# One written order for the last unit of a quantized FFN layer, and a changed order in its first units

## The chip, the cores and the metric

The kernel runs on one core of a Trainium2 chip. The metric is the device time of one execution in microseconds (us); a lower time is better. Times of before are the median of 3 runs; a separate execution was profiled, and all rows below come from that one.

## The reference

Two layers of an adapted feed-forward network work on x, 8 batches of 128 tokens with 512 features. What matters here is the second half of the second layer: a gated feed-forward part whose weights are 4-bit integers with one scale for each output row and each group of 128 inputs.

```python
def dequant(q, s, g=G):                       # G = 128
    O, In = q.shape
    return (q.reshape(O, In // g, g).astype(s.dtype) * s[:, :, None]).reshape(O, In)
...
Wg, Wu, Wd = dequant(gate_q, gate_s), dequant(up_q, up_s), dequant(down_q, down_s)
gate_score = jax.nn.silu(jnp.einsum('bsh,ih->bsi', x, Wg))      # I = 1792, H = 512
intermediate = gate_score * jnp.einsum('bsh,ih->bsi', x, Wu)
return jnp.einsum('bsi,hi->bsh', intermediate, Wd)
...
x = x + _L1_ffn_ref(_L1_cond_ref(x, itok_B_0_23, ...), ...)
```

## The kernel before

Features lie on the 128 partitions and tokens along the free axis: a tile is 128 x 1024, and a half of it (512 tokens, called tb 0 or 1) fills one PSUM bank. The last layer starts from h, the output of the adapter in front of it. h is held as two parts, `hi` (ACT rounds it, L1237) and `lo` (DVE takes the rest, L1239), so that each product needs two matmuls. Its halves come in the order in which the adapter finishes them; the last is chunk 3 of the first 512 tokens.

The 1792 inner features are cut into 14 units f of 128 (`NF`). For each unit there are 4 gate groups (s = 0, k = 0 to 3), 4 up groups (s = 1) and 4 down groups (o = 0 to 3). As the scales belong to groups of 128 inputs, each group is a PSUM result of its own, scaled while it is read out:

- `gate_or_up` (L1320 on): a pair of banks (`pair`), two halves with `hi` and `lo`, so 4 matmuls (`summed`, L1301). The first of a sum is read out by ACT (`scaled`, L1307), the others by DVE, which adds to the sum (L1310). Gate groups 0 and 1 go into one sum, 2 and 3 into another, which POOL adds (`gate_added`).
- `silu` on ACT (L1368), the product with the up sum on POOL (`gated_q`), the rounded part `act_hi` on ACT (`first_bits`, L1377) and the rest `act_lo` on POOL (`rest`). Every POOL operation is recorded at the helper `added`, L1316.
- `down_group` (L1342 on): 4 matmuls of `act_hi` and `act_lo`; DVE adds the scaled result to x (L1310), or ACT writes it to y (L1307) and POOL adds y to x (`y_added`).

Down groups belong to the unit two back (`LAG` = 2). Everything is issued with `in_order`, so each engine's list is the order of the Python text; an engine waits at the head of its list. Four pairs of banks go round: a group's first matmul waits until the group four back has been read out.

Units 0 to 12 run whole (L1386 to L1415). Inside a unit: gate 0, silu of the unit before (only f = 1 and 2), gate 1 (in unit 0: gate 2), `gated_q` of the unit before, down 0, gate 2, then `first_bits` and `rest` of the unit before, gate 3, `gate_added`, down 1, up 0 to 2, down 3 (by ACT and POOL), silu, up 3, down 2. POOL also issues the loads of later weights (L1193, L1195) between its operations.

The last unit (f = 13, L1419 on) runs in halves, each group in one bank of a second pool of 8 (`single`): first all 8 groups of tb 0, with the down groups of unit 11 between them, then all 8 of tb 1, then the down groups of unit 12, then those of unit 13, first tb 0 and then tb 1. x[o] of each half is stored (L1488) after its down group of unit 13: five stores by SP and three by ACT.

Of the kernel before, what the change touches and what calls it, by code (L numbers as in the profile page):

```python
# [7 lines left out]
F32 = mybir.dt.float32  # L8
# [3 lines left out]
ALU = mybir.AluOpType  # L12

P = 128
NB = 8
T = 1024
TB = 512
NTB = T // TB
G = 32
# [3 lines left out]
KC = H // P  # L23
R = 16
# [4 lines left out]
NF = FF // P  # L29
# [5 lines left out]
WARM = 2  # L35
NS = H + NF * P
LAG = 2


@with_exitstack  # L40
def kernel(
# [25 lines left out]
    nc = tc.nc  # L67

    nc_mm = nc.tensor.matmul
    in_order = tc.keep_in_program_order  # L70
# [40 lines left out]
    x = [const.tile([P, T], F32, tag=f"x{k}", name=f"x{k}") for k in range(KC)]  # L111
# [228 lines left out]
    ready = {}  # L340
# [164 lines left out]
    acts = {}  # L505
# [359 lines left out]
    with ExitStack() as top:  # L865
# [233 lines left out]
        first, then, last = scaling(1)  # L1099
# [41 lines left out]
    for sign in (1, -1):  # L1141
        in_order(
            nc.gpsimd.affine_select(
                out=one, in_=one, pattern=[[-sign, P]], compare_op=ALU.is_ge,
# [7 lines left out]
    sg = early.tile([P, NF, 2, KC], F32, tag="sg", name="sg")  # L1152
    sd = early.tile([P, KC, NF], F32, tag="sd", name="sd")
# [15 lines left out]
    b1 = gather_b(early, "1", l_bm, b1_rows, H)  # L1169
# [31 lines left out]
    whole, halves = slice(0, T), [bass.ts(tb, TB) for tb in range(NTB)]  # L1201
# [61 lines left out]
    for m in two:  # L1263
# [4 lines left out]
            fresh={(1, 1)}, go_on={(0, 0)},  # L1268
# [23 lines left out]
    def pair(name: str):  # L1292
        return pairs.tile([P, NTB, TB], F32, tag="pair", name=name)


    sums = {}

    def summed(ps, w, src, at):
        for n, part in enumerate(src):
            in_order(  # L1300
                nc.tensor.matmul(ps, w, part[:, at], start=(n == 0), stop=(n == len(src) - 1))  # L1301
            )

    def scaled(to, ps, scale, plus=None):

        if plus is None:
            in_order(nc.scalar.activation(to, ps, AF.Identity, scale=scale))  # L1307
        else:
            in_order(
                nc.vector.scalar_tensor_tensor(  # L1310
                    to, ps, scale, plus, op0=ALU.mult, op1=ALU.add
                )
            )

    def added(to, a, b, op):
        in_order(nc.gpsimd.tensor_tensor(to, a, b, op))  # L1316

    def unit_tile(what: str, f: int, bufs: int, dtype=F32):
        return l1.tile([P, T], dtype, tag=what, name=f"{what}_{f}", bufs=bufs)

    def gate_or_up(f: int, s: int, k: int, at=whole, into=None):


        on_act = k == 0 or (s == 0 and k == 2)
        if on_act and (f, s, k) not in sums:
            sums[f, s, k] = unit_tile(f"sum{s}{k}", f, 2)
        to = sums[f, s, k - k % 2 if s == 0 else 0][:, at]
        w, src = ready["q", f][0][:, s, k, :], [part[k] for part in parts]
        if into is None:
            both = pair(f"gu{s}_q{f}_{k}")  # L1330
            for tb in range(NTB):
                summed(both[:, tb], w, src, halves[tb])
            ps = both.rearrange("p b s -> p (b s)")
        else:
            summed(into, w, src, at)
            ps = into
        scaled(to, ps, sg[:, f, s, k : k + 1], None if on_act else to)

    def gate_added(f: int, at=whole):
        added(sums[f, 0, 0][:, at], sums[f, 0, 0][:, at], sums[f, 0, 2][:, at], ALU.add)  # L1340

    def down_group(f: int, o: int, on_act=False, at=whole, into=None):  # L1342
        w, src, scale = ready["q", f][1][:, bass.ts(o, P)], acts["q", f], sd[:, o, f : f + 1]
        if into is None:
            both = pair(f"d_q{f}_{o}")
            for tb in range(NTB):
                summed(both[:, tb], w, src, halves[tb])
            ps = both.rearrange("p b s -> p (b s)")
        else:
            summed(into, w, src, at)  # L1350
            ps = into
        to = x[o][:, at]
        if on_act:
            if (f, o) not in ys:
                ys[f, o] = unit_tile("y", f"{f}_{o}", 2)
            scaled(ys[f, o][:, at], ps, scale)
        else:
            scaled(to, ps, scale, to)

    ys = {}  # L1360

    def y_added(f: int, o: int, at=whole):
        added(x[o][:, at], x[o][:, at], ys[f, o][:, at], ALU.add)

    def silu(f: int, at=whole):
        if ("sil", f) not in sums:
            sums["sil", f] = unit_tile("sil_q", f, 2)
        in_order(nc.scalar.activation(sums["sil", f][:, at], sums[f, 0, 0][:, at], AF.Silu))  # L1368

    def gated_q(f: int, at=whole):  # L1370
        if ("q", f) not in acts:
            acts["q", f] = [unit_tile(f"act_{w}", f, 3, F32R) for w in ("hi", "lo")]
        up = sums[f, 1, 0][:, at]
        added(up, up, sums["sil", f][:, at], ALU.mult)

    def first_bits(f: int, at=whole):
        in_order(nc.scalar.copy(acts["q", f][0][:, at], sums[f, 1, 0][:, at]))  # L1377

    def rest(f: int, at=whole):
        hi, lo = acts["q", f]  # L1380
        added(lo[:, at], sums[f, 1, 0][:, at], hi[:, at].bitcast(F32), ALU.subtract)
# [4 lines left out]
    for f in range(NF - 1):  # L1386
        d = f - LAG
        if d > 0 and d - 1 + QBUFS < NF:
            load_q(d - 1 + QBUFS)
        gate_or_up(f, 0, 0)  # L1390
        if 0 < f <= LAG:
            silu(f - 1)
        gate_or_up(f, 0, 1 if f else 2)
        if f:
            gated_q(f - 1)
        if d >= 0:
            down_group(d, 0)
        gate_or_up(f, 0, 2 if f else 1)
        if f:
            first_bits(f - 1)  # L1400
            rest(f - 1)
        gate_or_up(f, 0, 3)
        gate_added(f)
        if d >= 0:
            down_group(d, 1)
        for k in range(3):
            gate_or_up(f, 1, k)
        if d >= 0:
            down_group(d, 3, True)
            y_added(d, 3)  # L1410
        if f >= LAG:
            silu(f)
        gate_or_up(f, 1, 3)
        if d >= 0:
            down_group(d, 2)  # L1415
# [2 lines left out]

    in_pairs.close()  # L1419
    last = ctx.enter_context(  # L1420
        tc.tile_pool(name="last", bufs=8, space=bass.MemoryType.PSUM, reuse_waits="tile")
    )

    def single(name: str):
        return last.tile([P, TB], F32, tag="bank", name=name)

    def down_half(f: int, o: int, tb: int, on_act: bool):
        down_group(f, o, on_act, halves[tb], single(f"d_q{f}_{o}_{tb}"))

    def down_halves(f: int, o: int, on_act: bool):  # L1430
        for tb in range(NTB):
            down_half(f, o, tb, on_act)

    def y_halves_added(f: int, o: int):
        for at in halves:
            y_added(f, o, at)

    f = NF - 1

    def half_unit(s: int, k: int, tb: int):  # L1440
        gate_or_up(f, s, k, halves[tb], single(f"gu{s}_q{f}_{tb}_{k}"))

    at = halves[0]
    for s in range(2):
        for k in range(KC):
            half_unit(s, k, 0)
            if (s, k) == (0, 1):
                gated_q(f - 1)
            if (s, k) == (0, 2):
                first_bits(f - 1)  # L1450
                rest(f - 1)
            if (s, k) == (0, 3):
                gate_added(f, at)
            if k % 2 == 1:
                o = 2 * s + k // 2
                down_halves(f - LAG, o, o == 1)
                if o == 1:
                    y_halves_added(f - LAG, o)
            if (s, k) == (1, 0):
                silu(f, at)  # L1460
    gated_q(f, at)

    d, at = f - 1, halves[1]
    for k in range(KC):
        half_unit(0, k, 1)
    gate_added(f, at)
    half_unit(1, 0, 1)
    silu(f, at)  # L1470
    half_unit(1, 1, 1)
    first_bits(f, halves[0])
    rest(f, halves[0])
    half_unit(1, 2, 1)
    half_unit(1, 3, 1)
    gated_q(f, at)
    down_halves(d, 1, True)
    down_halves(d, 0, False)
    first_bits(f, at)
    rest(f, at)  # L1480
    y_halves_added(d, 1)
    down_half(d, 3, 0, True)
    y_added(d, 3, halves[0])
    down_half(d, 3, 1, False)
    down_halves(d, 2, False)

    def store(engine, o: int, tb: int):
        in_order(engine.dma_start(out=out[:, o, halves[tb]], in_=x[o][:, halves[tb]]))  # L1488

    for o in (1, 0, 2, 3):  # L1490
        down_half(f, o, 0, o == 1)
        if o == 1:
            y_added(f, o, halves[0])
        else:
            store(nc.sync, o, 0)
    for n, o in enumerate(range(KC)):
        down_half(f, o, 1, False)
        if n == 0:
            store(nc.scalar, 1, 0)
        store(nc.scalar if n % 2 else nc.sync, o, 1)  # L1500


# [94 lines left out]
```

## Time and profile before

| what | value |
|---|---|
| runs | 709.4, 709.48, 707.73 us (median 709.4) |
| profiled execution | 707.46 us |
| its span | 705.7 us, 6850 instructions |
| mean granted TensorE clock | 0.994 |
| last layer's first matmul to its last eviction | 532.31 to 701.68 us of the span |
| last store's data ends | about 704.05 us |

The span is what the trace covers; the profiled execution is 1.76 us longer. A row of the timeline gives start, duration, engine, line, operation, output <- inputs, count, and in brackets how long the engine was idle before it and what released it. PE is TensorE, PEld its weight loads, DVE VectorE, POOL GpSimd, ACT ScalarE, SP the engine that issues most DMAs. A row with x4 covers four operations: its duration runs from the first one's start to the last one's end. A matmul here takes 0.39 us, but the next one starts 0.2268 us after it, since they are pipelined. A few matmuls at the very end (behind 698.16) are missing from the trace.

### The profile page before, as it was taken

How to read it: one execution, taken by the hardware profiler on the slowest of the kernel's cores; microseconds unless marked ns; L12 is line 12 of the kernel's file. 1: busy time of each engine (PE TensorE's matmuls, PEld its weight loads, DVE VectorE, ACT ScalarE, POOL GpSimd, SP SyncE). 2: the span in 40 equal slices, each digit the busy share in tenths (PEclk: the TensorE clock that was granted, in tenths of full speed). 3: DMA queues.
4: the chain of work that ended last, by engine and by line, in shares of the span. 5: the costliest groups of instructions: out<-in, count | busy, mean ns of one | idle time of the engine just before them, and what ended most of it. 6: DMA issues, size and time to landing. Idle time of an engine off the chain costs nothing. (4 is left out here: it accounts for less than half of the span.)

```text
span 705.7 us, 6850 instructions
## 1 busy us (share of the span) xinstructions
PE 676.7 (96%) x2400; PEld 381.8 (54%) x2400; DVE 445.4 (63%) x636; ACT 185.3 (26%) x273; POOL 370.6 (53%) x324
## 2 busy tenths in 40 slices
PE   8999999999999899898899899999999999999993
PEld 3444444444444345565566564444436677788872
DVE  6545344346242678687696479452447788999985
ACT  1221121110100012322333320000024655565642
POOL 5357666140001072955865748025203889898885
PEclk9999999999999999999999999999999999999998
DMA  6501234030002010220200050004900120000003
GB/s 228 188 1 51 76 124 169 1 134 1 1 0 104 1 61 29 90 89 1 90 1 0 16 175 25 0 0 118 329 1 30 41 79 16 15 1 1 0 1 119
DMA packets 18333, 42.46 MB, mean 60 GB/s; under 512 B 3118, under 2 KB 4286, under 8 KB 18172
## 3 DMA queue, kind: packets, MB, share of 16 engines
q1 hardware_dynamic: 11628, 25.44, 10.2%
q0 software_dynamic: 5376, 14.49, 6.6%
q10 hardware_dynamic: 1296, 2.10, 0.8%
q8 instruction: 19, 0.31, 0.2%
q14 instruction: 14, 0.11, 0.1%
HBM read 39.93 MB, written 2.10 MB: 60 GB/s over the span
## 5 line engine op out<-in xcount | busy, mean ns | idle before, releaser
L1310 DVE SCALAR_TENSOR_TENSOR sum<-gu_q,sg,sum 128x1024 f32<-128x1024 f32 (+1 forms) x75 | 90.4, 1211 | 20.0 <-ACT sum L1307 15.3
L1301 PE MATMUL gu_q<-h_hi,wgu_q 128*128 128x512 f32 x224 | 88.8, 396 | 3.1 <-DVE x L1310 1.6
L1301 PE MATMUL gu_q<-h_lo,wgu_q 128*128 128x512 f32 x224 | 87.5, 390 | 0.3 <-DVE h_lo L1239 0.3
L1310 DVE SCALAR_TENSOR_TENSOR x<-d_q,sd,x 128x1024 f32<-128x1024 f32 (+1 forms) x51 | 54.3, 1086 | 4.0 <-POOL x L1316 4.0
L73 PE MATMUL p_f<-T_h,s_f 128*128 128x512 f32 x112 | 52.9, 603 | 2.2 <-DVE T_h L319 2.2
L1307 ACT ACTIVATE sum<-gu_q,sg 128x1024 f32<-128x1024 f32 (+1 forms) x45 | 47.3, 1056 | 23.3 <-PE gu_q L1301 23.2
L1316 POOL TENSOR_TENSOR sum<-sum,sum 128x1024 f32<-128x1024 f32 (+1 forms) x15 | 33.9, 2262 | 36.6 <-DVE sum L1310 36.0
L1301 PEld LDWEIGHTS gu_q<-h_hi,wgu_q 128*128 128x128 f32 x224 | 42.0, 188 | 17.4 <-DVE x L1310 4.6
L1301 PE MATMUL d_q<-act_hi,wd_q 128*128 128x512 f32 x112 | 44.7, 399 | 3.6 <-ACT y L1307 3.2
L1301 PEld LDWEIGHTS gu_q<-h_lo,wgu_q 128*128 128x128 f32 x224 | 42.1, 188 | 8.9 <-DVE h_lo L1239 0.6
L1301 PE MATMUL d_q<-act_lo,wd_q 128*128 128x512 f32 x112 | 44.0, 392 | 0.3 <-POOL act_lo L1316 0.3
L1316 POOL TENSOR_TENSOR act_lo<-sum,act_hi 128x1024 fp32r<-128x1024 f32 (+1 forms) x15 | 33.8, 2256 | 18.0 <-ACT act_hi L1377 16.7
L73 PE MATMUL p_c<-x,raw_c 128*128 128x512 f32 x88 | 42.7, 606 | 0.5 <-DMA x<-in_xT_dram 0.5
L73 PE MATMUL p_c<-T_x,raw_c 128*128 128x512 f32 x88 | 41.6, 594 | 0.2 <-DVE T_x L319 0.2
L73 PE MATMUL p_c<-T_x,s_c 128*128 128x512 f32 x88 | 41.2, 592 | 0.0
L570 DVE TENSOR_TENSOR act_c<-p_c,v_c 128x512 f32<-128x512 f32 x11 | 7.6, 691 | 52.3 <-PE p_c L73 52.3
L73 PE MATMUL p_f<-h,raw_f 128*128 128x512 f32 (+1 forms) x96 | 40.2, 541 | 0.1
L73 PE MATMUL d_f<-act_f,ds_f 128*128 128x512 f32 x84 | 36.6, 593 | 0.0
L73 PE MATMUL d_f<-act_f,wd_f 128*128 128x512 f32 x84 | 36.4, 592 | 0.0
L685 POOL TENSOR_TENSOR h<-h,dv_c 128x512 f32<-128x512 f32 x2 | 2.5, 1267 | 62.9 <-ACT dv_c L682 62.9
L1316 POOL TENSOR_TENSOR sum<-sum,sil_q 128x1024 f32<-128x1024 f32 (+1 forms) x15 | 33.9, 2261 | 2.7 <-ACT sil_q L1368 2.7
L1316 POOL TENSOR_TENSOR x<-x,y 128x1024 f32<-128x1024 f32 (+1 forms) x17 | 34.1, 2015 | 0.0
(276 smaller groups left out, 1265.3 us busy)
## 6 DMA issues: line engine op xcount, KB each, us to landing
raw_f<-in_f_gu_dram SPq DMA_DIRECT2D x14, 512.0 KB
wgu_q<-in_q_gu_dram POOLq DMA_DIRECT2D x14, 512.0 KB, 7.5
raw_c<-in_c_gu_dram SPq DMA_DIRECT2D x10, 512.0 KB
wd_f<-in_f_down_dram SPq DMA_DIRECT2D x14, 256.0 KB
wd_q<-in_q_down_dram POOLq DMA_DIRECT2D x14, 256.0 KB, 7.0
x<-in_xT_dram SPq DMA_DIRECT2D x11, 256.0 KB
wd_c<-in_c_down_dram SPq DMA_DIRECT2D x11, 256.0 KB
x<-in_xT_dram ACTq DMA_DIRECT2D x5, 256.0 KB
```

Of the source, the lines that this page charges most:

```text
L73: in_order(nc_mm(*args, **kwargs))
L570: add(act[0], x4, v, ALU.add)
L685: nc.gpsimd.tensor_tensor(at(m + 2, 1), at(m + 2, 1), v[m], ALU.add)
L1301: nc.tensor.matmul(ps, w, part[:, at], start=(n == 0), stop=(n == len(src) - 1))
L1307: in_order(nc.scalar.activation(to, ps, AF.Identity, scale=scale))
L1310: nc.vector.scalar_tensor_tensor(to, ps, scale, plus, op0=ALU.mult, op1=ALU.add)
L1316: in_order(nc.gpsimd.tensor_tensor(to, a, b, op))
```

## The change

Three things change, all in the last layer. The number of matmuls is the same.

1. In unit 0, up group 0 is issued ahead of gate group 3, and gate group 3 takes tb 1 before tb 0 (`turned`).
2. In unit 1, `first_bits` and `rest` of unit 0 move from behind gate 2 to behind up 2. On ACT `act_hi` then comes after the read-out of up 0; on POOL `act_lo` comes after the gate addition of unit 1.
3. The last unit, with all down groups of units 11, 12 and 13, is one written list. Matmul groups (`g`, `d`) and read-outs (`G`, `D`, `y`) are separate steps, so that a read-out may stand far behind its group. Numbers are tb, s, k for gate and up, and units back, o, tb for down. Eight banks are taken by turns in the order 0, 1, 2, 3, 6, 7, 4, 5. For tb 0 all four gate groups go into one sum (no POOL addition). A half of x is stored when its third contribution is in, so a down group of unit 13 need not be its last one: eight stores, the fifth and seventh issued by ACT and six by SP. DVE reads out 29 half groups instead of 28.

```diff
+LAST = """
+g100 g102 G102 g110 g103 G103 g111 G110 d231 G111 G100 g101 G101 g000 D231 M g001 g002 G000 d230
+g112 G001 d221 B +1 s1 g113 g010 d211 D230 G112 G002 G010 g011 G113 G011 g013 R g012 m1 y211
+D221 g003 b1 d201 Y211 G012 d131 d220 r1 G003 d120 G013 d210 d011 s0 D220 D131 d031 y210 m0 D201
+d101 b0 D120 Y210 D011 D031 d121 d130 y130 D121 d021 r0 Y130 d110 D021 d111 d001 d020 D101 y110
+y111 d010 y010 Y110 D001 D020 Y111 d100 D100 d030 d200 d000 D030 Y010 D200 D000
+"""
...
-        if f:
+        if f > 1:
             first_bits(f - 1)
             rest(f - 1)
-        gate_or_up(f, 0, 3)
+        if f == 0:
+            gate_or_up(f, 1, 0)
+        gate_or_up(f, 0, 3, f == 0)
         gate_added(f)
...
-        for k in range(3):
+        for k in range(0 if f else 1, 3):
             gate_or_up(f, 1, k)
+        if f == 1:
+            first_bits(f - 1)
+            rest(f - 1)
...
+    turns = [last.tile([P, TB], F32, tag=f"bank{n}", name=f"bank{n}") for n in range(8)]
...
+    def next_bank(key, w, src, at):
+        n = len(groups)
+        ps = turns[(0, 1, 2, 3, 6, 7, 4, 5)[n % 8]]
+        groups[key] = ps
+        summed(ps, w, src, at)
...
+    def store(o: int, tb: int):
+
+        waiting[o, tb] -= 1
+        if waiting[o, tb] == 0:
+            left.append((o, tb))
+            engine = nc.scalar if len(left) > 4 and len(left) % 2 else nc.sync
+            in_order(engine.dma_start(out=out[:, o, halves[tb]], in_=x[o][:, halves[tb]]))
...
+    steps = {
+        "g": gate_up_half, "G": gate_up_out, "d": down_half, "D": down_out, "y": down_copied,
+        "Y": down_added, "+": lambda tb: gate_added(last_f, halves[tb]),
+        "s": lambda tb: silu(last_f, halves[tb]), "m": lambda tb: gated_q(last_f, halves[tb]),
+        "b": lambda tb: first_bits(last_f, halves[tb]), "r": lambda tb: rest(last_f, halves[tb]),
+        "M": lambda: gated_q(last_f - 1), "B": lambda: first_bits(last_f - 1),
+        "R": lambda: rest(last_f - 1),
+    }
+    for step in LAST.split():
+        steps[step[0]](*(int(c) for c in step[1:]))
```

More of the change, by code (lines that the diff above doesn't have):

```diff
@@ L1319, in unit_tile, with gate_or_up @@
         return l1.tile([P, T], dtype, tag=what, name=f"{what}_{f}", bufs=bufs)
-    def gate_or_up(f: int, s: int, k: int, at=whole, into=None):
+    def gate_or_up(f: int, s: int, k: int, turned=False):
         on_act = k == 0 or (s == 0 and k == 2)
@@ L1326, in gate_or_up @@
             sums[f, s, k] = unit_tile(f"sum{s}{k}", f, 2)
-        to = sums[f, s, k - k % 2 if s == 0 else 0][:, at]
+        to = sums[f, s, k - k % 2 if s == 0 else 0]
         w, src = ready["q", f][0][:, s, k, :], [part[k] for part in parts]
[L1329 to L1336, printed above, removed]
+        both = pair(f"gu{s}_q{f}_{k}")
+        for tb in reversed(range(NTB)) if turned else range(NTB):
+            summed(both[:, tb], w, src, halves[tb])
+        ps = both.rearrange("p b s -> p (b s)")
         scaled(to, ps, sg[:, f, s, k : k + 1], None if on_act else to)
@@ L1340, in gate_added, with down_group @@
         added(sums[f, 0, 0][:, at], sums[f, 0, 0][:, at], sums[f, 0, 2][:, at], ALU.add)
-    def down_group(f: int, o: int, on_act=False, at=whole, into=None):
+    def down_group(f: int, o: int, on_act=False):
         w, src, scale = ready["q", f][1][:, bass.ts(o, P)], acts["q", f], sd[:, o, f : f + 1]
[L1344 to L1352, printed above, removed]
+        both = pair(f"d_q{f}_{o}")
+        for tb in range(NTB):
+            summed(both[:, tb], w, src, halves[tb])
+        ps = both.rearrange("p b s -> p (b s)")
+        to = x[o]
         if on_act:
-            if (f, o) not in ys:
-                ys[f, o] = unit_tile("y", f"{f}_{o}", 2)
-            scaled(ys[f, o][:, at], ps, scale)
+            ys[f, o] = unit_tile("y", f"{f}_{o}", 2)
+            scaled(ys[f, o], ps, scale)
         else:
@@ L1360, with y_added @@
     ys = {}
-    def y_added(f: int, o: int, at=whole):
-        added(x[o][:, at], x[o][:, at], ys[f, o][:, at], ALU.add)
+    def y_added(f: int, o: int):
+        added(x[o], x[o], ys[f, o], ALU.add)
     def silu(f: int, at=whole):
@@ L1420 @@
     last = ctx.enter_context(
-        tc.tile_pool(name="last", bufs=8, space=bass.MemoryType.PSUM, reuse_waits="tile")
+        tc.tile_pool(name="last", bufs=1, space=bass.MemoryType.PSUM, reuse_waits="tile")
     )
[L1424 to L1443, printed above, removed]
-    for s in range(2):
[L1445 to L1493, printed above, removed]
-        else:
[L1495 to L1500, printed above, removed]
+    turns = [last.tile([P, TB], F32, tag=f"bank{n}", name=f"bank{n}") for n in range(8)]
@@ new lines, with gate_up_half @@
+    last_f = NF - 1
+    for s in range(2):
+        for k in (0, 2) if s == 0 else (0,):
+            sums[last_f, s, k] = unit_tile(f"sum{s}{k}", last_f, 2)
+    groups, left, y_halves = {}, [], []
+    waiting = {(o, tb): 3 for o in range(KC) for tb in range(NTB)}
+    def next_bank(key, w, src, at):
[3 more added lines that the diff above has]
+        summed(ps, w, src, at)
+    def gate_up_half(tb: int, s: int, k: int):
+        w = ready["q", last_f][0][:, s, k, :]
+        next_bank(("g", tb, s, k), w, [part[k] for part in parts], halves[tb])
@@ new lines, in gate_up_out, with down_half @@
+    def gate_up_out(tb: int, s: int, k: int):
+        apart = s == 0 and k >= 2 and tb == 1
+        to = sums[last_f, s, 2 if apart else 0][:, halves[tb]]
+        fresh = k == 0 or apart and k == 2
+        ps = groups["g", tb, s, k]
+        scaled(to, ps, sg[:, last_f, s, k : k + 1], None if fresh else to)
+    def down_half(back: int, o: int, tb: int):
+        f = last_f - back
+        next_bank(("d", back, o, tb), ready["q", f][1][:, bass.ts(o, P)], acts["q", f], halves[tb])
+    def store(o: int, tb: int):
[4 more added lines that the diff above has]
+            in_order(engine.dma_start(out=out[:, o, halves[tb]], in_=x[o][:, halves[tb]]))
@@ new lines, in down_out, with down_copied @@
+    def down_out(back: int, o: int, tb: int):
+        to = x[o][:, halves[tb]]
+        f = last_f - back
+        scaled(to, groups["d", back, o, tb], sd[:, o, f : f + 1], to)
+        store(o, tb)
+    def down_copied(back: int, o: int, tb: int):
+        n = len(y_halves)
+        if n % 2 == 0:
+            y_halves.append(unit_tile("y", f"last_{n}", 2))
+        else:
+            y_halves.append(y_halves[-1])
+        ys[back, o, tb] = y_halves[-1][:, halves[n % 2]]
+        f = last_f - back
+        scaled(ys[back, o, tb], groups["d", back, o, tb], sd[:, o, f : f + 1])
@@ new lines, in down_added @@
+    def down_added(back: int, o: int, tb: int):
+        to = x[o][:, halves[tb]]
+        added(to, to, ys[back, o, tb], ALU.add)
+        store(o, tb)
+    steps = {
[6 more added lines that the diff above has]
+    }
```

## The prediction

> **What bounds the kernel now.** I read the page first (engine shares), then the busy time of each engine by stretches of the last layer, then the timeline around each idle time of TensorE (PE), then the stores. The page, and the table of stretches (columns: length, then busy time and count of PE, weight loads, DVE, ACT, POOL, granted clock, DMA share, GB/s):
>
> ```profile
> PE 676.7 (96%) x2400; PEld 381.8 (54%) x2400; DVE 445.4 (63%) x636; ACT 185.3 (26%) x273; POOL 370.6 (53%) x324
> ```
>
> ```profile
> 614.00:673.30 59.30, 59.30 (x263) 49.08 (x262) 54.41 (x45) 35.13 (x34) 52.52 (x23) 1.00 0.00 1
> 673.30:690.00 16.70, 14.74 (x63) 11.22 (x61) 13.48 (x19) 8.62 (x14) 13.27 (x8) 1.00 0.00 1
> 690.00:702.00 12.00, 5.39 (x18) 3.06 (x18) 7.73 (x12) 2.98 (x5) 8.71 (x7) 0.95 0.30 110
> ```
>
> From 614 to 673.3 PE never rests: a unit is 48 matmuls at 0.2268 us start to start, 10.88 us. Only outside this stretch can an order of work gain. The reader is to see the two places. **The end**, from the timeline:
>
> ```profile
> 675.55 0.50 PE L1301 MATMUL gu_q<-h_hi,wgu_q 128*128 128x512 f32 x1 [1.63 <-DVE x L1310]
> 689.66 4.69 DVE L1310 SCALAR_TENSOR_TENSOR x<-d_q,sd,x 128x512 f32<-128x512 f32 x7
> 690.56 0.50 PE L1301 MATMUL d_q<-act_hi,wd_q 128*128 128x512 f32 x1 [0.89 <-ACT y L1307]
> 694.54 4.95 POOL L1316 TENSOR_TENSOR x<-x,y 128x512 f32<-128x512 f32 x4
> 697.82 0.50 PE L1301 MATMUL d_q<-act_hi,wd_q 128*128 128x512 f32 x1 [1.73 <-ACT y L1307]
> 698.30 3.38 DVE L1310 SCALAR_TENSOR_TENSOR x<-d_q,sd,x 128x512 f32<-128x512 f32 x5 [3.96 <-POOL x L1316]
> ```
>
> The second bank of the last unit is that of the down pair which DVE reads until 675.50, so PE waits 1.63. At the very end DVE waits 3.96 for POOL, whose four additions into x stand in one row behind act_lo; five evictions then run to 701.68. **The beginning of the layer** (first unit f=0, then f=1):
>
> ```profile
> 536.07 0.50 PE L1301 MATMUL gu_q<-h_hi,wgu_q 128*128 128x512 f32 x1 [0.74 <-ACT h_hi L1237]
> 536.86 0.50 PE L1301 MATMUL gu_q<-h_lo,wgu_q 128*128 128x512 f32 x1 [0.28 <-DVE h_lo L1239]
> 544.56 2.40 POOL L1316 TENSOR_TENSOR sum<-sum,sil_q 128x1024 f32<-128x1024 f32 x1 [2.02 <-ACT sil_q L1368]
> 548.12 2.39 POOL L1316 TENSOR_TENSOR act_lo<-sum,act_hi 128x1024 fp32r<-128x1024 f32 x1 [1.16 <-ACT act_hi L1377]
> 549.11 0.50 PE L1301 MATMUL gu_q<-h_hi,wgu_q 128*128 128x512 f32 x1 [0.40 <-ACT sum L1307]
> 550.48 2.39 POOL L1316 TENSOR_TENSOR sum<-sum,sum 128x1024 f32<-128x1024 f32 x1
> 554.06 2.41 POOL L1316 TENSOR_TENSOR sum<-sum,sil_q 128x1024 f32<-128x1024 f32 x1 [0.64 <-ACT sil_q L1368]
> ```
>
> After this POOL runs its four whole-width operations a unit at 2.36 each, plus one wait of 1.16 and DMA issues of 0.57 to 0.60: the act_lo rows of units 2 to 5 start at 569.44, 581.28, 592.54, 603.83, that is 11.84, 11.26 and 11.29 apart, more than PE's 10.88. So until 613.65 PE is held back again and again (idle gaps of 0.15 to 0.35) by banks that come free late, and where it stands at 614 is set by when POOL's row of units began. When the DMA issues end, POOL's period is 10.67, and PE is alone the bound.
>
> **The first unit.** The added up group (4 matmuls, 0.91) is moved work; nothing is added. Now PE stands 0.89 and 0.56 before the last gate group, whose h comes last. In the new order the up group takes the fourth pair of banks, free when DVE's last l_v ends at 535.26: it starts at about 535.33 and ends at 536.35. But the last gate group is now the fifth and takes the first pair, which ACT reads from 535.93 to 537.04, behind the last h_hi. This is an added wait, 0.78 by these rows; the group starts at 537.1 and ends at 538.1, where before both groups ended at 538.58. By then both halves of h are there, so the turned order costs nothing. Gain on PE 0.45, not 1.45.
>
> **Unit 1.** POOL's product of unit 0 starts 0.46 earlier too (its silu stands on ACT behind unit 1's first group), at 544.1. Then before: product 2.36, idle 1.16, act_lo, sum, DMA issue, idle 0.64, next product at 554.06. In the new order act_hi follows the up evictions, and the sum of unit 1 stands ahead of act_lo: product, sum, act_lo (3 x 2.36) and one issue of 0.6 without idle: next product at 551.8 to 551.9. Gain 1.8 there, 2.2 with the 0.46. What it costs: act_lo of unit 0 ends at 551.2 instead of 550.51, and the first down group, which PE reaches at 549.9, waits 1.2 for it with all of PE behind it. That lo matmul then starts at 551.4 (before: 552.16), still ahead, and this wait takes the place of those at 549.11 to 551.82 (1.2 and restarts). As POOL's row decides until 614, **2.2** reach the last unit. Bounds: 0 (the wait for act_lo or a later one eats it) and 3.0 (2.2, and the gaps before 614 shrink as well); I take 2.2 because laying the old order out with the same durations puts PE's last wait at 613.40, against 613.31.
>
> **The last unit**, on the old axis. Work is the same: 80 matmuls (18.1), DVE 29 evictions (one more than now), POOL 11 halves at 1.23 and two wholes at 2.36 (18.3), ACT 16 short ones. One eviction on DVE costs 0.66 start to start (the x7 row: 3.95 over 6), 0.74 long; where it needs the result just before it, 0.78. The first bank turn skips the pair DVE holds until 675.50, so the 1.63 wait goes, but DVE is only free at 675.42 anyway. I then laid out the written order engine by engine, each operation after its own engine and its operands (0.48 from a last matmul's start to its reader, 0.07 between engines). DVE never waits for a bank's matmul: 675.42 + 25 x 0.66 + 3 x 0.78 + 0.74 = **695.0**, against 701.68 now, 6.7 less. The same working on the old order gives 701.75. Covers: PE waits 0.46 for a bank at 682.8, 0.22 at 686.8 and 0.80 at 690.9, each a reader still in DVE's row, so nobody waits on; thinnest slack ahead of DVE is 0.02 to 0.13 (third, fifth and tenth operation), so 0.1 more on each hand-over costs some 0.1, not a sum. If the cover fails, everything is behind the waiting eviction: DVE's list has no other work. POOL's additions of y end at 693.9, and the last eviction needs none.
>
> **Stores.** Eight of 256 KB as before, now six on SP, two on ACT at the end of its list. Now six of them share the last stretch:
>
> ```profile
> GB/s 0 0 0 0 0 0 0 0 0 133 399 358 379 420 358 420 348 369 379 389 379 389 410 328 389 430 348 379 420 358 82 0 0 0 0 0 0 0 0 0
> ```
>
> These are 0.2 us slices from 698: issue at 699.08, data from 699.93 (0.85 later) to 704.05, six at 0.69; the span ends 1.65 later. In the new order the issues fall at 688.8, 690.2, 691.6, 692.3, 692.7, 693.6, 693.9, 695.06; the last one's data ends at 696.62, the span at 698.27. So the tail gains 705.7 - 698.27 = **7.4**, of which 0.7 is this queue.
>
> **Sum.** 7.4 + 2.2 = 9.6: span 696.1. The profiled execution took 707.46, 1.76 over its span, so 697.8 on its own scale. It lies 1.94 under the median of the runs shown (707.73 to 709.48); carried to the median, 709.4 - 9.6 = **699.8**.
>
> **Rivals.**
> 1. The head (units 0 and 1) gives nothing: the first down group's wait for act_lo, or a bank wait behind it, uses up the 2.2. For it: the wait is new, and PE arrives 1.3 early. Against: POOL's idle of 1.80 is real and goes. 702.0. Chance 0.13.
> 2. DVE's row runs at 0.755 instead of 0.66 (the stretch of five sums at 685.97 took 3.77, its operations waiting on one another's results): DVE ends at 697.3, the span at 700.6, tail 5.1: 702.1. Against: the order alternates its targets. Chance 0.14; with rival 1 0.03 (704.3).
> 3. The change does not do what it says: the bank order still meets DVE's pair, PE stands until 675.55 at the second group; DVE's first new eviction, which reads the fourth, comes 1.9 later and the row with it: 701.7. Chance 0.03.
> 4. Slower: DVE and POOL cannot work at once where both are full. Then the tail is 19.6 + 18.3 behind 675.42, DVE ends at 713.3, 718 in all. It decides from about 11.7 of POOL's 18.3 us being excluded. Against it: from 614 to 673.3 both together were busy 54.41 + 52.52 in 59.30 us, so at least 47.6 overlapped, and the x7 row ran at 0.66 beside a busy POOL. Chance 0.03.
>
> The Trainium skill ("Trainium Architecture - The Big Picture", What this means for kernel authors) says that VectorE and GpSimd contend for a shared port pair, and that it is an exclusive lock; taken flatly that is rival 4. Its "GPSIMD Engine Reference" (Specifications) limits the contention to VectorE instructions in a 2-port mode or with two SBUF inputs; the evictions read one operand from PSUM, and the trace's 47.6 us agree with the narrower rule.
>
> **How the numbers follow.** Forecast 0.62, rivals as above, 0.02 for losses not named. About 0.3% (2.1 us) is what a measurement tells from no change. Faster by more: all but rival 4 and the unnamed, 0.95; same 0.02 (the unnamed); slower 0.03 (rival 4). The range runs from 697.3 (profiled scale, and the higher bound of the head in part) to 702.4 (rivals 1, 2, 3 each alone); left out are about 0.1 of cases.
>
> **What would show it.** Right: PE's idle at 675.55 gone; DVE's last 29 evictions about 19.6 us with hardly an idle; span minus DVE's end about 3.3; POOL without the 1.16 and 0.64 between the first two products; PE's last head stall 2.2 earlier. Wrong: DVE idle in its last row (then the releaser names the failed cover), evictions over 0.7 apart, or the last unit starting less than 1.5 earlier.

## The result and the profile after

The changed kernel took **699.94 us** (median of 4 runs, 699.58 to 701.17), the kernel before 709.41 (4 runs, 707.73 to 709.48): ratio **0.9875**, 95% interval 0.9856 to 0.9894. Forecast was 699.8. The profiled execution took 699.98, its span 698.26. The two medians do not stand at the same place among their runs: before has 707.73 beside three at 709.40 to 709.48, after three at 699.58 to 699.98 beside 701.17, and between the low runs of each the difference is 7.8 us.

To compare stages, two points of time serve from here on. **L** is the first matmul of the last layer: nothing ahead of it was changed. **U** is the start of DVE's last whole down read-out, the last thing ahead of the new list.

| us | before | after | gain |
|---|---|---|---|
| L | 532.31 | 532.69 | -0.38 |
| L to POOL's first product | 12.25 | 11.88 | 0.37 |
| L to POOL's second product | 21.75 | 19.56 | 2.19 |
| L to U | 141.91 | 139.76 | 2.15 |
| U to DVE's first half read-out | 2.20 | 1.20 | 1.00 |
| DVE's row of half read-outs | 25.27 (28) | 19.79 (29) | 5.48 |
| U to the last store's data | 29.83 | 22.60 | 7.23 |
| U to the span's end | 31.51 | 25.81 | 5.70 |
| L to the span's end | 173.42 | 165.57 | **7.85** |

So the median moved 9.47, but the changed part of the program only 7.85, and the data was out 7.23 earlier where the span ended 5.70 earlier. Both gaps are taken up below.

The page of after, and the table of stretches with the columns of the one before (the middle stretch begins 1.35 ahead of U, in before 0.92):

```profile
PE 675.0 (97%) x2400; PEld 382.5 (55%) x2400; DVE 446.1 (64%) x637; ACT 185.2 (27%) x272; POOL 369.0 (53%) x323
```

```profile
611.80:671.10 59.30, 59.30 (x263) 49.06 (x263) 54.51 (x44) 35.46 (x33) 52.06 (x22) 1.00 0.00 1
671.10:687.80 16.70, 16.43 (x71) 12.85 (x70) 16.49 (x25) 10.44 (x16) 16.64 (x12) 1.00 0.01 1
687.80:697.00 9.20, 3.25 (x14) 2.02 (x12) 5.44 (x8) 1.32 (x3) 4.57 (x4) 0.92 0.61 228
```

In the first stretch PE never rests, as before. In the second DVE goes from 13.48 to 16.49 busy and POOL from 13.27 to 16.64, of 16.70 each: both are now full. Apart from one read-out, what was added is not work but a list in which neither waits. The timeline of after's end:

```profile
672.45 1.27 DVE L1325 SCALAR_TENSOR_TENSOR x<-d_q,sd,x 128x1024 f32<-128x1024 f32 x1
673.65 2.08 DVE L1325 SCALAR_TENSOR_TENSOR sum<-bank,sg,sum 128x512 f32<-128x512 f32 x3
682.90 10.55 DVE L1325 SCALAR_TENSOR_TENSOR x<-bank,sd,x 128x512 f32<-128x512 f32 x15
687.35 5.02 POOL L1331 TENSOR_TENSOR x<-x,y_last 128x512 f32<-128x512 f32 x4
689.16 0.50 PE L1316 MATMUL bank<-act_hi,wd_q 128*128 128x512 f32 x1 [0.67 <-DVE x L1325]
```

Where before had PE idle for 1.63 and DVE for 3.96, no DVE row has a bracket at all: from 672.45 it runs through to 693.45. PE now waits for DVE (0.67 at 689.16), and neither DVE nor POOL waits for PE; only ACT does, which was busy for 10.44 of the 16.70. The beginning of the layer in after:

```profile
537.45 0.50 PE L1316 MATMUL gu_q<-h_hi,wgu_q 128*128 128x512 f32 x1 [0.56 <-ACT sum L1322]
544.57 2.40 POOL L1331 TENSOR_TENSOR sum<-sum,sil_q 128x1024 f32<-128x1024 f32 x1 [1.53 <-ACT sil_q L1374]
546.93 2.41 POOL L1331 TENSOR_TENSOR sum<-sum,sum 128x1024 f32<-128x1024 f32 x1
549.30 2.39 POOL L1331 TENSOR_TENSOR act_lo<-sum,act_hi 128x1024 fp32r<-128x1024 f32 x1
551.74 0.50 PE L1316 MATMUL d_q<-act_lo,wd_q 128*128 128x512 f32 x1 [0.98 <-POOL act_lo L1331]
552.25 2.41 POOL L1331 TENSOR_TENSOR sum<-sum,sil_q 128x1024 f32<-128x1024 f32 x1
```

POOL goes from one product to the next without a wait (before: 1.16 and 0.64), and PE pays with the wait for act_lo of unit 0 that the working had put in.

### The profile page after: what moved, and what is told of

It reads as the page before. It is cut to its first block, busy times and chain, and to the rows that moved or that the text cites. A ratio compares the mean times of both kernels' runs of the same rounds, so it can differ in the third digit from the quotient of the medians.

```text
span 698.3 us, 6852 instructions
## 1 busy us (share of the span) xinstructions
PE 675.0 (97%) x2400; PEld 382.5 (55%) x2400; DVE 446.1 (64%) x637; ACT 185.2 (27%) x272; POOL 369.0 (53%) x323
## 3 DMA queue, kind: packets, MB, share of 16 engines
q1 hardware_dynamic: 11772, 25.71, 10.6%
## 4 chain that ended last, share of the span: by engine, by line
PE 78%; POOL 11%; DVE 5%; issue 3%; ACT 1%; POOLq 0%; DVEq 0%; ACTq 0%
PE p_c L88 21%; PE gu_q L1316 12%; PE d_f L88 12%; PE d_c L88 10%; PE p_f L88 6%; PE d_q L1316 6%; PE l L88 4%; POOL s L308 4%; DVE r_f L972 2%; POOL s_f L308 2%; PE za_f L88 2%; POOL s L301 1%; PE zb_f L88 1%; PE bank L1316 1%; POOL s_f L301 1%
## 5 line engine op out<-in xcount | busy, mean ns | idle before, releaser
L1325 DVE SCALAR_TENSOR_TENSOR sum<-gu_q,sg,sum 128x1024 f32<-128x1024 f32 x65 | 83.1, 1283 | 14.1 <-ACT sum L1322 10.5
L1316 PE MATMUL gu_q<-h_hi,wgu_q 128*128 128x512 f32 x208 | 82.0, 394 | 0.6 <-ACT sum L1322 0.6
L1316 PE MATMUL gu_q<-h_lo,wgu_q 128*128 128x512 f32 x208 | 81.1, 390 | 0.0
L1322 ACT ACTIVATE sum<-gu_q,sg 128x1024 f32<-128x1024 f32 x39 | 43.2, 1113 | 24.1 <-PE gu_q L1316 24.0
L1316 PEld LDWEIGHTS gu_q<-h_hi,wgu_q 128*128 128x128 f32 x208 | 39.0, 188 | 12.6 <-DVE x L1325 2.1
L1316 PEld LDWEIGHTS gu_q<-h_lo,wgu_q 128*128 128x128 f32 x208 | 39.1, 188 | 7.8
L1325 DVE SCALAR_TENSOR_TENSOR x<-d_q,sd,x 128x1024 f32<-128x1024 f32 x33 | 42.1, 1275 | 0.3 <-PE d_q L1316 0.3
L1316 PE MATMUL d_q<-act_lo,wd_q 128*128 128x512 f32 x88 | 34.4, 391 | 1.0 <-POOL act_lo L1331 1.0
L586 POOL TENSOR_TENSOR act_c<-act_c,p_c 128x512 f32<-128x512 f32 x10 | 12.8, 1275 | 41.6 <-DVE act_c L585 33.0
L1316 PE MATMUL d_q<-act_hi,wd_q 128*128 128x512 f32 x88 | 34.6, 394 | 0.0
```

The lines of the kernel that those rows point to most:

```text
L586: mul(act[0], act[0], p1, ALU.mult)
L1325: nc.vector.scalar_tensor_tensor(to, ps, scale, plus, op0=ALU.mult, op1=ALU.add)
```

## The experiments

The theory after the result: the head gives 2.15, through POOL's row; the tail's row of DVE runs as laid out; and the end is held by something that the prediction did not have. Its rivals: that the head's gain is chance of the execution; that the span's end goes with the stores as before.

**One half of the change alone.** head_only is the kernel before with the edits to units 0 and 1; tail_only is after with these lines turned back to the old ones, so that only the written list is new:

```diff
 head_only, against before
-        if f:
+        if f > 1:
             first_bits(f - 1)
             rest(f - 1)
-        gate_or_up(f, 0, 3)
+        if f == 0:
+            gate_or_up(f, 1, 0)
+        gate_or_up(f, 0, 3, turned=f == 0)
...
-        for k in range(3):
+        for k in range(0 if f else 1, 3):
             gate_or_up(f, 1, k)
+        if f == 1:
+            first_bits(f - 1)
+            rest(f - 1)
```

> The old tail with the two changes in units 0 and 1. Theory (POOL's row of units starts earlier): the last unit's first read-out on DVE comes 2.2 us earlier after the layer's first matmul than before (139.7 instead of 141.9 us), and the tail behind it stays at 31.5 us, so the time is 2.2 us under before (707.2 against a median of 709.4). Rival (the new wait for act_lo uses the gain up): 0 to 0.5 us.

Measured: L to U 139.77 (before 141.91), so 2.14; U to the span's end 31.18 (31.51), 0.33. Median 707.13 (10 runs, 703.76 to 707.31) beside 708.25 of before (15 runs, 706.65 to 710.09), ratio 0.9968, interval 0.9953 to 0.9983: 1.2 to 3.3 us, which holds the 2.47 of the stages. The head came as expected, but the tail did not stay as it was. In head_only the second group of the old list no longer waits for the pair that DVE reads last:

```profile
674.41 0.50 PE L1301 MATMUL gu_q<-h_hi,wgu_q 128*128 128x512 f32 x1 [0.43 <-DVE sum L1310]
680.85 0.75 DVE L1310 SCALAR_TENSOR_TENSOR sum<-gu_q,sg,sum 128x512 f32<-128x512 f32 x1 [2.54 <-ACT sum L1307]
```

PE waits 0.43 there instead of 1.63, and DVE's first half read-out comes 1.19 behind U instead of 2.20. Yet only 0.33 of this is left at the end, as DVE's next wait, for ACT, grows from 1.99 to 2.54. The same 1.19 stands in unit1_only below and the old 2.20 in unit0_only, so it comes with unit 1's edit; why the second bank is another one there is open.

> The old units 0 and 1 with the written last unit. Theory (the tail is bound by DVE's row, and then by POOL's last operation, whose drain record ends 4.67 us after it): from the last whole down read-out on DVE to the end of the span 25.8 us, as with both parts, instead of 31.5; time 5.6 us under before on the scale of the profiles. Rival (the two parts help each other): less than 4.5 us, as the tail starts from another state of the engines.

Measured: L to U 141.94, unchanged; U to the span's end 26.36, so 5.15: 0.55 less than both parts together give there, and above the rival's 4.5. Median 702.62 (4 runs, 702.47 to 704.86), ratio 0.9913, interval 0.9893 to 0.9933. By stages 2.47 + 5.15 = 7.62; together they give 7.85. The halves add up but for 0.23: with the old head DVE's first half read-out comes 1.46 after U and its row takes 20.09, with the new one 1.20 and 19.79.

**The kernel before once more,** unchanged, to see how far one execution differs from another:

> The kernel of before once more, for a second profile. Theory (the difference between the runs at 707.5 and at 709.4 lies ahead of the last layer or behind the last store, not in the stages that the change touches): from the layer's first matmul to the last read-out again 169.4 us within 0.3. Rival: the stages themselves take up to 1.9 us more.

Measured: time 709.27, L 534.17. From L on it is the same execution: U 141.88 behind L, the first and second product 12.25 and 21.74, the end 31.53 behind U, L to the end 173.41. The whole 1.86 lies ahead of L. The stretch from 240 to 420 us, before and then before_again (columns as in the table of stretches):

```profile
240.00:420.00 180.00, 169.99 (x599) 105.14 (x598) 130.11 (x189) 50.85 (x111) 111.59 (x128) 0.99 0.14 48
```

```profile
240.00:420.00 180.00, 170.00 (x596) 104.78 (x595) 128.24 (x185) 50.85 (x111) 110.32 (x126) 0.98 0.13 45
```

In the same 180 us the second shows fewer instructions on PE, DVE and POOL alike (596 for 599, 185 for 189, 126 for 128), at a granted clock of 0.98 instead of 0.99. Every comparison below is therefore made from L or from U. L was 532.3 to 534.9 over all profiled executions of this study.

**The head's two edits apart.** unit0_only has the up group ahead of gate group 3 and the turned order, unit1_only only the move of `first_bits` and `rest`:

```diff
 unit0_only, against before
-        gate_or_up(f, 0, 3)
+        if f == 0:
+            gate_or_up(f, 1, 0)
+        gate_or_up(f, 0, 3, turned=f == 0)
...
-        for k in range(3):
+        for k in range(0 if f else 1, 3):
```

> The kernel of before with the up group ahead of gate group 3 and the turned halves in unit 0 alone. Theory (the new bank wait takes most of it back): POOL's first product starts 0.4 to 0.5 us earlier after the layer's first matmul than before (12.25 us), and the last unit starts 0.4 to 0.5 earlier. Rival (what PE stood before is gained in full): 1.3 to 1.45 us.

```diff
 unit1_only, against before
-        if f:
+        if f > 1:
             first_bits(f - 1)
             rest(f - 1)
...
+        if f == 1:
+            first_bits(f - 1)
+            rest(f - 1)
```

> The kernel of before with act_hi and act_lo of unit 0 moved behind up 2 of unit 1 alone. Theory (POOL's idle of 1.80 us between its first two products goes): the second product starts 1.8 us earlier after the layer's first matmul than before (21.75 us), the last unit 1.7 to 1.8 us earlier. Rival (PE's wait for act_lo eats it): 0 to 0.5 us.

These two, and all kernels below but pool_short, ran once; they are compared by their stages, which two executions of before gave alike within 0.03 us. Measured, L to U: 141.47 with unit 0's edit (gain 0.44), 140.10 with unit 1's (gain 1.81). They add to 2.25, against 2.15 for both. The product of unit 0 starts 0.36 earlier with the first edit and not at all with the second (12.26).

**Which of the two lists carries unit 1's gain?** The move of `first_bits` and `rest` changes ACT's list (act_hi behind the read-out of up 0) and POOL's (act_lo behind the gate addition). My theory was that POOL's order is what counts; each kernel here keeps one of the two.

```diff
 pool_order, against after: ACT's list as before, POOL's as after
-        if f > 1:
+        if f:
             first_bits(f - 1)
+        if f > 1:
             rest(f - 1)
...
         if f == 1:
-            first_bits(f - 1)
             rest(f - 1)
```

> As the changed kernel, but in unit 1 only act_lo is moved (POOL's list as in the changed kernel); act_hi stays where it was before, ahead of the read-out of up group 0 on ACT. Theory (the order on POOL is what counts): POOL's second product starts at 19.5 to 19.7 us after the layer's first matmul, as in the changed kernel, and the last unit within 0.3 us of it. Rival (ACT's order is what counts: the read-out of up 0 stands 1 us behind act_hi, and PE and DVE with it): the last unit 1 us or more later than in the changed kernel.

Measured: L to U 140.82, so 1.06 of the gain is lost, and POOL's second product starts 20.63 behind L, not 19.5 to 19.7. The theory was incomplete. pool_order's timeline:

```profile
546.73 1.05 ACT L1383 CAST act_hi<-sum 128x1024 fp32r<-128x1024 f32 x1 [1.52 <-POOL sum L1331]
547.69 1.10 ACT L1322 ACTIVATE sum<-gu_q,sg 128x1024 f32<-128x1024 f32 x1
548.85 0.50 PE L1316 MATMUL gu_q<-h_hi,wgu_q 128*128 128x512 f32 x1 [0.40 <-ACT sum L1322]
553.04 2.41 POOL L1331 TENSOR_TENSOR sum<-sum,sil_q 128x1024 f32<-128x1024 f32 x1 [1.10 <-DVE sum L1325]
```

POOL's list is right, and yet its second product stands 1.10 idle, for the up sum of DVE. The chain runs back through ACT: act_hi waits there for POOL's product (1.52), the read-out of up 0 stands behind it, so its bank comes free late, PE waits, and the up groups end late.

```diff
 act_order, against after: ACT's list new, POOL's gate addition behind act_lo
-        gate_added(f)
+        if f != 1:
+            gate_added(f)
...
         if f == 1:
             first_bits(f - 1)
             rest(f - 1)
+            gate_added(f)
```

> The complement of the run in which only act_lo moved: as the changed kernel, but the gate addition of unit 1 on POOL is put behind act_lo of unit 0, so POOL's list is the old one, and ACT's is the new one (act_hi behind the read-out of up 0). Theory (both lists are needed): act_lo waits for act_hi about 1.2 us after the first product, and the second product starts at about 21.4 us after the layer's first matmul instead of 19.56; the last unit starts 1.3 to 1.9 us later than in the changed kernel. Rival (ACT's list alone gives the gain): within 0.3 us of the changed kernel.

Measured: L to U 141.61, so 1.85 is lost, all of what unit 1 gives. act_order's POOL:

```profile
548.17 2.41 POOL L1331 TENSOR_TENSOR act_lo<-sum,act_hi 128x1024 fp32r<-128x1024 f32 x1 [1.20 <-ACT act_hi L1383]
554.13 2.37 POOL L1331 TENSOR_TENSOR sum<-sum,sil_q 128x1024 f32<-128x1024 f32 x1 [0.66 <-ACT sil_q L1374]
```

The waits of before (1.16 and 0.64) are back. With ACT's new list alone nothing of unit 1's gain is left, with POOL's alone about 0.75 of the 1.81; the whole gain needs both. In each of these kernels U moves with POOL's second product, within 0.05 us.

**The first bank turn.** bank_met lets the second group of the new list take a bank of the pair that DVE still reads, which is the prediction's third rival:

```diff
-        ps = turns[(0, 1, 2, 3, 6, 7, 4, 5)[n % 8]]
+        ps = turns[(0, 4, 5, 1, 2, 3, 6, 7)[n % 8]]
```

> As the changed kernel, but the banks go 0, 4, 5, 1, 2, 3, 6, 7, so that the second group of the last unit meets the pair that DVE still reads, as before. Theory (DVE is the bound, its first read-out takes the fourth group): PE stands about 1.6 us at the second group, DVE's row starts 1.9 us later and ends about 1.9 later, the span grows by 1.5 to 1.9. Rival (PE has room, DVE's row is not the bound): under 0.5 us.

Measured: the end is 27.77 behind U instead of 25.81, 1.96 later, a little more than the 1.5 to 1.9 expected. bank_met's timeline:

```profile
673.77 0.50 PE L1316 MATMUL bank<-h_hi,wgu_q 128*128 128x512 f32 x1 [1.62 <-DVE x L1325]
675.58 2.11 DVE L1325 SCALAR_TENSOR_TENSOR sum<-bank,sg,sum 128x512 f32<-128x512 f32 x3 [1.86 <-PE bank L1316]
```

PE's old 1.63 is back as 1.62, DVE's first half read-out comes 1.94 later, and the row behind it is the same (19.81 against 19.79): a full row keeps every delay of its start. So in the new list the bank order is worth 1.96 of the tail's 5.70. In the old list, whose row has waits of its own, losing nearly the same wait gave 0.33 (head_only above).

**What holds the end?** The last store's data ends at about 695.05 in after: DMA throughput in slices of 0.1 us from 692.

```profile
GB/s 512 369 328 369 369 389 328 492 348 369 369 328 430 451 389 348 348 389 389 430 348 389 164 267 430 389 369 369 389 348 103 0 0 0 0 0 0 0 0 0
```

The span ends at 698.26, 3.2 later; before it was 1.68 (704.05 to 705.73). The rows of the closing line give count, then min/median/max in ns, then first and last start. Before, and then what SP waits for there (total, times, longest, us):

```profile
L1592 POOLq DRAIN  x3: 46/97/6353, 697.8 to 705.2; - x3
...
SPq L1592 <- DMA out_dram<-x: 2.7, 5, 0.6
SPq L1592 <- PEq L1592: 1.0, 2, 0.8
```

After:

```profile
L1594 POOLq DRAIN  x3: 46/245/6310, 690.7 to 698.0; - x3
...
SPq L1594 <- PEq L1594: 2.5, 2, 1.6
SPq L1594 <- DMA out_dram<-x: 1.2, 2, 0.6
```

POOL's closing DRAIN is recorded for 6.31 us, from 690.73 to 697.04. SP, done with its stores at about 695.6, then stands 1.6 in the closing barrier (before 0.8). The row names PE's sequencer as the releaser, but PE's last matmul was over before 693; what is late is POOL, as the next two kernels show. In before the same DRAIN ended at 704.16, 0.44 ahead of the last store's completion at 704.60, and was hidden. In all the kernels here it ends 4.66 to 4.67 us behind POOL's last operation (always a half addition into x), at whatever time that ends. The Trainium skill ("Perfetto Trace Analysis", Sequencer-only Instruction (DRAIN, etc)) has the record of such an instruction begin when its semaphores are satisfied, so by that page the 6.31 is no wait for another engine; the constant distance of 4.66 to 4.67 from POOL's own last operation agrees with it. What fills these 4.67 us is open.

That makes a test. pool_short gives one of POOL's additions of y at the end to DVE instead (one read-out more on DVE, one addition fewer on POOL and one copy fewer on ACT):

```diff
-y111 d010 y010 Y110 D001 D020 Y111 d100 D100 d030 d200 d000 D030 Y010 D200 D000
+y111 d010 Y110 D001 D020 Y111 d100 D100 d030 d200 d000 D030 D010 D200 D000
```

> As the changed kernel, but the down group of unit 13 for o = 1, tb 0 is added to x by DVE instead of ACT and POOL, so POOL has one operation less at its very end and DVE one more. Theory (the end of the span hangs on POOL's last operation plus 4.67 us): POOL ends 1.25 us earlier, DVE 0.66 later, the stores' last completion about 0.7 later; then the stores are last again and the span shrinks by about 0.9 us (697.4 against 698.3). Rival (the end hangs on the last store alone, and the longer stretch behind it is chance): the span grows by 0.7 us.

| us from U | after | pool_short | two_left_out |
|---|---|---|---|
| DVE's row ends | 20.99 | 21.64 | 20.26 |
| POOL's last operation ends | 19.92 | 18.66 | 19.82 |
| POOL's DRAIN ends | 24.58 | 23.33 | 24.49 |
| stores complete (SP) | 23.14 | 23.75 | 22.83 |
| span ends | 25.81 | 25.03 | 25.71 |

DVE ends 0.65 later, the stores 0.61 later, and yet the span ends **0.78 earlier**, because POOL ends 1.26 earlier. That can't be if the stores held the end. In pool_short they do again: 23.75 and 1.28 for the barrier, with the DRAIN 0.42 ahead of them. Its closing rows:

```profile
L1594 POOLq DRAIN  x3: 97/193/7322, 688.7 to 697.3; - x3
...
SPq L1594 <- DMA out_dram<-x: 1.2, 1, 1.2
SPq L1594 <- PEq L1594: 1.1, 2, 0.9
```

The median is 699.43 (5 runs, 699.07 to 701.12), ratio to before 0.9878, interval 0.9858 to 0.9899. From L to the end it is the shortest kernel here (164.75 against 165.57), but in the medians 0.5 us between it and after is not told apart.

two_left_out is the opposite test, a shorter list of DVE with POOL's untouched; it leaves out two of the down contributions of unit 11:

```diff
-        scaled(to, groups["d", back, o, tb], sd[:, o, f : f + 1], to)
+        if (back, o, tb) not in ((2, 3, 0), (2, 2, 0)):
+            scaled(to, groups["d", back, o, tb], sd[:, o, f : f + 1], to)
```

> As the changed kernel, but two read-outs of DVE are left out (unit 11's down groups o = 3 and o = 2 of tb 0 are not added to x; their matmuls run). Theory now (POOL's list is as full as DVE's, and POOL's last operation plus 4.67 us ends the span): DVE ends 0.7 to 1.3 us earlier, POOL only 0.1 to 0.3, and the span behind the start of the last unit shrinks from 25.81 by no more than 0.3. Rival (the theory of the prediction: DVE's row alone decides the tail): it shrinks by 1.3 us.

Its timeline at the end:

```profile
682.90 9.89 DVE L1325 SCALAR_TENSOR_TENSOR x<-bank,sd,x 128x512 f32<-128x512 f32 x14
687.34 5.02 POOL L1331 TENSOR_TENSOR x<-x,y_last 128x512 f32<-128x512 f32 x4
```

DVE ends 0.73 earlier, POOL, in the same place, 0.10, and the span 0.10. So it is POOL's list that sets the end of after, not DVE's. Taking two read-outs from DVE gave 0.10; taking one addition from POOL gave 0.78, until the stores held the end again.

## Why the prediction was right, and where it was not

The mechanisms of the head and of DVE's row were the predicted ones; that of the program's end was not. The time on the median's scale was hit within 0.2 us, but that was luck: the sum itself was 1.75 too high, 9.6 where the changed part gained 7.85.

- **Unit 0.** Forecast 0.45; alone it gives 0.44. The added bank wait of 0.78 is PE's row at 537.45: 0.56 idle in the bracket, 0.72 against matmuls 0.2268 apart.
- **Unit 1.** Forecast 1.8; alone 1.81. The new wait for act_lo, forecast at 1.2, is 1.13 (0.98 in the bracket, with the restart). PE's last stall of the head comes 2.14 earlier behind L (611.55 against 613.31), and the whole head gives 2.15 of the 2.2 foreseen. That POOL's row decides until 614 held: U moved with POOL's second product in every kernel that changes the head. What the prediction's words "POOL's idle goes" left out is shown by pool_order: without ACT's new order POOL gets an idle time of another origin, 1.10.
- **The bank order.** It does what was said; bank_met prices it at 1.96, where the prediction had 1.9 for its third rival. That unit 1's edit alone would take the old list off this pair it did not foresee.
- **DVE's row.** Laid out at 19.6, measured 19.79: (19.79 - 0.74) / 28 = 0.68 start to start. The 25 steps priced at 0.66 took 0.66. The three where an operation adds to the result of the one just before it (D021, D001 and the last, D000) took 0.84 each, not 0.78, and that is the missing 0.2. The row of five sums before holds two such steps of 0.85 and two of 0.66, so its mean of 0.755 hid their price. The new row starts 1.20 behind U as laid out, and ends 6.48 earlier, not 6.7. The data of the last store ends 7.23 earlier, not 7.43; the same 0.2.
- **The stores' term is the step that failed:** "the span ends 1.65 later". That was carried over from before, where the last store's completion released the barrier. In after the data ends and the span ends 3.2 later, since POOL's DRAIN takes the stores' place (pool_short and two_left_out). The mis-sized term is the tail: 7.4 forecast, 5.70 measured; 1.5 of the difference is this wait, 0.2 the row. A hint stood in the trace of before: POOL's long DRAIN, 6353 ns from 697.8, ends only 0.44 ahead of the last store's completion, so this cover was thin. The prediction moved the stores 7.4 and POOL's last operation 5.6 (699.49 to 693.9) earlier by its own numbers, and did not ask what else waits for POOL.
- **POOL beside DVE.** The prediction took DVE's row as the tail's bound and POOL's additions as ended in time. In after they are in time for x, but not for the end of the program.
- **The remaining 1.6 of the median's move** is no gain that the stages show. The execution of before that was read took 707.46, 1.94 under the median from which the prediction took its 9.6; after's median, 699.94, lies beside its profiled execution, 699.98. So the medians compare unlike executions. Where such a difference can lie is shown by before's two profiled executions, 707.46 and 709.27: all of it stands ahead of L. No trace shows where L stood in the runs at 709.4. The hit within 0.2 us is thus two errors that cancel: a gain 1.75 too high in the stages, and 1.62 that came from the runs. On the profiled scale the forecast was 697.8 and the measured execution 699.98, that is the 1.75 and an L that came 0.38 later. The interval of the ratio, 7.5 to 10.2 us, holds 7.85 as well as 9.47. After and its five variants had L from 532.4 to 533.0, the kernels with the old head or the old tail from 532.3 to 534.9. Whether the program has any part in that is open; no run here tells it.

**The rivals.** The head that gives nothing (702.0) fell by unit0_only and unit1_only. DVE's row at 0.755 fell by the 0.68: in a list that alternates its targets only three steps cost more. The bank order that still meets DVE's pair is not what after does, and bank_met shows that it would have cost what was said. The slower case, DVE and POOL shutting each other out, fell plainly: in one stretch of 16.70 us DVE was busy for 16.49 and POOL for 16.64, so at least 16.43 overlapped, at the same 0.66 an operation. Of the two pages of the Trainium skill that were weighed, the narrower rule ("GPSIMD Engine Reference", Specifications) agrees with these rows; the exclusive lock taken for every operation does not.

## What to carry to other kernels

When an engine's last work moves, ask for every other engine when its last operation ends and what the program's end does with it: the closing of an engine that was hidden by 0.4 us becomes the bound as soon as the others move by more. A written order that moves one step moves it on every engine's list, and each list has to be priced by itself, as unit 1's gain needed both. A wait that is removed from a row with other waits can be lost at the next one (0.33 of about 1 us in head_only); in a full row it counts in full (1.96). Compare executions from the last point that the change leaves alone; a hit on the total can hold errors of the same size with opposite signs.

## What the runs showed of the hardware

- The closing DRAIN of GpSimd ended 4.66 to 4.67 us behind GpSimd's last operation in each of the profiled kernels here, and the span ended 1.22 to 1.23 us behind it where it was last. Where the stores were last, the span ended 1.13 to 1.28 us behind their completion as SP sees it.
- The same program reached the same point 1.86 us later in another execution (L 532.31 and 534.17), at a granted clock of 0.98 instead of 0.99 in the stretch from 240 to 420 us, and ran alike from there on within 0.03 us. That the clock made the whole difference is not shown.
- A half read-out on DVE (128x512, from PSUM) started 0.66 us after the one before it, and 0.84 to 0.86 after it where it added to the result that the one before had just written (three such steps in before, three in after).
- DVE's evictions from PSUM and POOL's additions in SBUF did not hold each other up even when both were full (16.49 and 16.64 us of 16.70).
